# Attention block on one core: softmax sums by 32x32 block transposes, 1/l broadcast through memory, first loads in another order

## The chip, the cores and the metric

One core of a Trainium2 chip runs the whole kernel. The metric is the device time of one execution in microseconds (us), the median of several. Engines are named as in the profile: PE (TensorE matmul), PEld (its weight loads), DVE (VectorE), ACT (ScalarE), POOL (GpSimd), SP (SyncE, here the queue that issues most DMAs).

## The reference

The input x is 16 images of 512 channels by 32x32 = 1024 positions, float32 throughout. For each image:

```
xn   = groupnorm(x; 8 groups) * gamma + beta
q,k,v = qkv_w @ xn + qkv_b            (4 heads of 128 channels)
attn = softmax_m(q^T k / sqrt(128))   (1024 x 1024 per head)
o    = attn @ v
out  = x + proj_w @ o + proj_b
```

## The kernel before, in words

Channels lie on the 128 partitions, positions along the free axis, so an image is four tiles x_b_0..3 of 128x1024. Every product is float32 with 512 moving columns; one such call appears in the trace as two MATMUL records.

The program is unrolled over `steps` = 16 images x 4 heads x 8 blocks of 128 keys. Step s computes in `scores` (L243) a score block of 128 keys x 1024 queries (two calls, L247), its exponential p on ACT (L252), and adds p to a running sum `tot` on DVE (L255, L257). In the same step `weighted_sum` (L274) adds the block before, s-1, into `po` in PSUM (L280). The softmax maximum is not subtracted; a flag computed at the end says whether the sums stayed in a safe range, and a slower general path runs only if they did not.

At the first step of the next head, `denominators` (L259) takes `tot` (128 keys-within-block x 1024 queries) and sums it over the partitions. It does so with a product against a 128x128 tile of ones (L264), two halves, so that the sum l of every query stands on all 128 partitions. DVE then computes 1/l on 128x512 twice (L266) and a check value `worst` twice (L269). When the last key block has been added, DVE multiplies `po` by 1/l into `o` (L288), which frees `po`.

`plan_head` (L309) spreads other work over a head's steps: the q and k products of the next head (`qk_unit`, L204), in head 0 the output projection of the image before (`proj_unit`, L226, from step 2) and the loads of the next image, in head 2 the group statistics of the next image (L38 to L64), in head 3 its normalisation (L69 on DVE, then the beta addition L72 on POOL, on DVE for the first image), its q, k of head 0 and its v (L216).

The Tile framework does not keep this order on each engine: it puts every engine's instructions in order when the kernel is built, from priorities that follow the order of the code and from its own estimate of when each is ready. An engine then runs its list strictly in that order. Tiles come from pools; PSUM has two score tiles of two banks (`ps_s`), one `po` of two banks (`ps_o`) and two one-bank accumulators (`ps_a`, tag acc) that q/k, v, projection and l all share.

At the start the four x tiles of image 0 are issued on SP's queue, gamma, beta and all weights (four tiles of 768 KB for q, k and v, then the projection) on ACT's queue. At the end come the flag and the eight projection units of the last image.

Of the kernel before, what the change touches and what calls it, by code (L numbers as in the profile page):

```python
# [26 lines left out]
class Norm:  # L27
# [36 lines left out]
        nc.vector.tensor_mul(sc, rstd, self.gamma)  # L64
        return mu, sc

    def apply(self, xn, x, mu, sc, c, eng):

        self.nc.vector.tensor_scalar(  # L69
            xn, x, mu[:, c : c + 1], sc[:, c : c + 1], ALU.subtract, ALU.mult  # L70
        )
        eng.tensor_scalar(xn, xn, self.beta[:, c : c + 1], None, ALU.add)  # L72


@with_exitstack
def attention_block(
    ctx: ExitStack,
    tc: tile.TileContext,
    x: bass.AP,
    gamma: bass.AP,  # L80
    beta: bass.AP,
    qkv_wT: bass.AP,
    qk_b: bass.AP,
    v_b: bass.AP,
    proj_wT: bass.AP,
    proj_b: bass.AP,
    out: bass.AP,
):
# [12 lines left out]
    avg = const.tile([P, P], F32, name="avg")  # L101
    neghalf = const.tile([P, NCC], F32, name="neghalf")
    ones = const.tile([P, P], F32, name="ones")
# [5 lines left out]
    wqkv = [const.tile([P, 3 * C], F32, name=f"wqkv_{c}") for c in range(NCC)]  # L109
    wproj = [const.tile([P, C], F32, name=f"wproj_{c}") for c in range(NCC)]  # L110

    spans = const.tile([P, B * HEADS * NH2], F32, name="spans")
    flag = const.tile([P, 1], I32, name="flag")

    with ExitStack() as fast:
        fast_path(
            fast, tc, x, (gamma, beta, qkv_wT, qk_b, v_b, proj_wT, proj_b), out,
            avg, neghalf, ones, gamma_sb, beta_sb, qkb_sb, vb_sb, projb_sb, wqkv, wproj,
            spans, flag, (B, C, N, NCC, NH2, NB, GC, SCALE),
        )  # L120
# [11 lines left out]
def fast_path(  # L132
    ctx, tc, x, sources, out, avg, neghalf, ones, gamma_sb, beta_sb, qkb_sb, vb_sb, projb_sb,
    wqkv, wproj, spans, flag, dims,
):

# [37 lines left out]
    nc.scalar.dma_start(vb_sb, v_b.to_broadcast((P, C)))  # L174
# [13 lines left out]

    def normalise(b, c):
        xns[b, c] = xnpool.tile([P, N], F32, tag="xn", name=f"xn_{b}_{c}")  # L190
        norm.apply(xns[b, c], xs[b, c], *scaled[b], c, nc.vector if b == 0 else nc.gpsimd)


    def qk_unit(b, h, which, half):

        store = (qs, ks)[which]
        if half == 0:
            store[b, h] = qkpool.tile(
                [P, N], F32, tag=f"qk{which}", name=f"qk{which}_{b}_{h}"
            )  # L200
        o = which * HEADS + h
        acc = ps_a.tile([P, HALF], F32, tag="acc", name=f"pqk_{b}_{h}_{which}_{half}")
        for c in range(NCC):
            nc.tensor.matmul(  # L204
                acc, wqkv[c][:, ts(o, P)], xns[b, c][:, ts(half, HALF)],
                start=(c == 0), stop=(c == NCC - 1),
            )
        nc.scalar.activation(  # L208
            store[b, h][:, ts(half, HALF)], acc, AF.Identity, bias=qkb_sb[:, o : o + 1]
        )  # L210

    def v_unit(b, j):

        acc = ps_a.tile([P, HALF], F32, tag="acc", name=f"pv_{b}_{j}")
        for c in range(NCC):
            nc.tensor.matmul(  # L216
                acc[:, :C], xns[b, c][:, ts(j, P)], wqkv[c][:, 2 * C : 3 * C],
                start=(c == 0), stop=(c == NCC - 1),
            )
# [3 lines left out]
    def proj_unit(b, o, half):  # L223
        acc = ps_a.tile([P, HALF], F32, tag="acc", name=f"pp_{b}_{o}_{half}")
        for c in range(NCC):
            nc.tensor.matmul(  # L226
                acc, wproj[c][:, ts(o, P)], os_[b, c][:, ts(half, HALF)],
                start=(c == 0), stop=(c == NCC - 1),
            )
        y = ypool.tile([P, HALF], F32, tag="y", name=f"y_{b}_{o}_{half}")  # L230
# [12 lines left out]
    def scores(s):  # L243
# [8 lines left out]
        nc.scalar.activation(ps[s], sc, AF.Exp, scale=SCALE)  # L252
# [6 lines left out]
    def denominators(b, h):  # L259

        t = tot.pop((b, h))
        for half in range(NH2):
            l = ps_a.tile([P, HALF], F32, tag="acc", name=f"l_{b}_{h}_{half}")
            nc.tensor.matmul(l, ones, t[:, ts(half, HALF)], start=True, stop=True)  # L264
            r = lpool.tile([P, HALF], F32, tag=f"rinv{half}", name=f"rinv_{b}_{h}_{half}")
            nc.vector.reciprocal(r, l)  # L266
            worst = lpool.tile([P, HALF], F32, tag="worst", name=f"worst_{b}_{h}_{half}")
            i = (b * HEADS + h) * NH2 + half
            nc.vector.scalar_tensor_tensor(  # L269
                worst, l, 1.0, r, ALU.mult, ALU.max, accum_out=spans[:, i : i + 1]  # L270
            )
            rinv[b, h, half] = r

    def weighted_sum(s):  # L274
        b, h, j = where(s)
# [68 lines left out]
    for s in range(steps + 1):  # L344
        if s < steps:
# [11 lines left out]
    total = gn.tile([P, 1], F32, tag="total", name="total")  # L357
    nc.vector.tensor_reduce(total, spans, AX.X, ALU.add)
    fine = gn.tile([P, 1], F32, tag="fine", name="fine")
    nc.vector.tensor_scalar(fine, total, LIMIT, None, ALU.is_le)  # L360
    nc.vector.tensor_scalar(flag, fine, -1.0, 1.0, ALU.mult, ALU.add)
    for u in proj_units(B - 1):
        u()


def general_path(
# [21 lines left out]
    with tc.For_i(0, B, 1) as b:  # L388
# [8 lines left out]
            norm.chunk(mv, xs[c], c)  # L397
        mu, sc = norm.group(mv)
        for c in range(NCC):
            norm.apply(xn[c], xs[c], mu, sc, c, nc.vector)  # L400
        for j in range(NB):
            acc = product(lambda c: xn[c][:, ts(j, P)], lambda c: wqkv[c][:, 2 * C : 3 * C])
            nc.vector.tensor_add(vs[j], acc, vb_sb)
        for h in range(HEADS):
            for w in range(2):
                i = w * HEADS + h
                for half in range(NH2):
                    acc = product(
                        lambda c: wqkv[c][:, ts(i, P)], lambda c: xn[c][:, ts(half, HALF)]
                    )  # L410
                    nc.scalar.activation(
                        q[w][:, ts(half, HALF)], acc, AF.Identity, bias=qkb_sb[:, i : i + 1]
# [76 lines left out]
```

## Time and profile before

| | us |
|---|---|
| median of 3 runs | 3697.14 (3696.3 to 3697.45) |
| the profiled execution's own time | 3696.41 |
| its span in the trace | 3694.5 |

| engine | busy us | share of the span |
|---|---|---|
| PE | 3654.3 | 99% |
| PEld | 1608.1 | 44% |
| DVE | 1470.9 | 40% |
| ACT | 701.1 | 19% |
| POOL | 200.2 | 5% |

The span begins with the first instruction of any engine and ends with the last. A PE record's time is modelled to its pipelined end, so records of a stream overlap: the time between starts tells what one costs.

### The profile page before, as it was taken

What the parts mean: (1) busy time and instruction counts of PE and PEld (TensorE: products, weight loads), DVE (VectorE), ACT (ScalarE), POOL (GpSimd) and SP (SyncE); (2) the same over time, 40 slices, a digit from 0 to 9 for tenths busy, and PEclk for the clock granted to TensorE, in tenths of its full rate; (3) what the DMA queues carried; (4) which work ended last, traced back from release to release, by engine and by line L of the source; (5) the groups of instructions that cost most, each with busy time, mean ns of one, the idle gap of its engine ahead of it and who ended that gap; (6) DMA issues with size and microseconds to landing.
All of it is one profiled execution on the core that took longest, in us unless ns stands there. A gap on an engine that the chain in (4) does not pass through costs nothing.

```text
span 3694.5 us, 20904 instructions
## 1 busy us (share of the span) xinstructions
PE 3654.3 (99%) x8512; PEld 1608.1 (44%) x8512; DVE 1470.9 (40%) x1596; ACT 701.1 (19%) x769; POOL 200.2 (5%) x80
## 2 busy tenths in 40 slices
PE   7999999999999999999999999999999999999998
PEld 3444444444444444444444444444444444444443
DVE  3334434434344343433434334353434434344334
ACT  1211212112121121211212112121211212112121
POOL 0010100101001010000101001010010100101000
PEclk9999999999999999999999999999999999999999
DMA  2001010010100101001010010100001000010000
GB/s 94 0 0 46 0 37 9 0 46 0 41 5 3 43 0 46 0 10 36 0 46 0 12 35 0 46 0 15 31 0 46 0 23 23 0 46 0 14 9 24
DMA packets 29621, 72.97 MB, mean 20 GB/s; under 512 B 3792, under 2 KB 3792, under 8 KB 29520
## 3 DMA queue, kind: packets, MB, share of 16 engines
q1 hardware_dynamic: 27648, 67.12, 5.3%
q10 hardware_dynamic: 1872, 4.47, 0.3%
q8 instruction: 68, 1.11, 0.1%
q14 instruction: 33, 0.27, 0.0%
HBM read 38.02 MB, written 33.55 MB: 19 GB/s over the span
## 4 chain that ended last, share of the span: by engine, by line
PE 92%; DVE 2%; POOL 0%; issue 0%; POOLq 0%
PE pqk L204 22%; PE po L280 22%; PE s L247 21%; PE pp L226 12%; PE pv L216 11%; PE l L264 3%; DVE xn L69 2%; DVE tot L257 0%; POOL rstd L62 0%; DVE rinv L266 0%; PE pv L58 0%; DVE sc L64 0%; DVE ve L60 0%; PE pm L47 0%; DVE y L231 0%
## 5 line engine op out<-in xcount | busy, mean ns | idle before, releaser
L280 PE MATMUL po<-p,v 128*128 128x512 f32 x2048 | 961.6, 593 | 0.0
L257 DVE TENSOR_TENSOR tot<-tot,p 128x1024 f32<-128x1024 f32 x384 | 470.2, 1225 | 1233.0 <-ACT p L252 1219.1
L247 PE MATMUL s<-qk,qk 128*128 128x512 f32 x2048 | 941.6, 592 | 0.0
L204 PE MATMUL pqk<-xn,wqkv 128*128 128x512 f32 x2048 | 925.4, 593 | 4.3 <-DVE xn L72 4.3
L252 ACT ACTIVATE p<-s 128x1024 f32<-128x1024 f32 x512 | 523.9, 1023 | 1949.5 <-PE s L247 1947.1
L204 PEld LDWEIGHTS pqk<-xn,wqkv 128*128 128x128 f32 x2048 | 389.9, 190 | 495.2 <-issue 474.9
L247 PEld LDWEIGHTS s<-qk,qk 128*128 128x128 f32 x2048 | 389.1, 190 | 489.8 <-issue 474.5
L280 PEld LDWEIGHTS po<-p,v 128*128 128x128 f32 x2048 | 386.8, 190 | 475.5 <-issue 456.1
L266 DVE RECIPROCAL rinv<-l 128x512 f32<-128x512 f32 x128 | 420.4, 3326 | 301.3 <-PE l L264 301.3
L226 PE MATMUL pp<-o,wproj 128*128 128x512 f32 x1024 | 457.3, 595 | 5.5 <-DVE worst L269 5.5
L216 PE MATMUL pv<-wqkv,xn 128*128 128x512 f32 x1024 | 449.4, 592 | 0.0
L208 ACT ACTIVATE qk<-pqk,qkb_sb 128x512 f32<-128x512 f32 x256 | 175.9, 687 | 978.6 <-PE pqk L204 978.6
L226 PEld LDWEIGHTS pp<-o,wproj 128*128 128x128 f32 x1024 | 195.6, 191 | 252.5 <-issue 241.7
L216 PEld LDWEIGHTS pv<-wqkv,xn 128*128 128x128 f32 x1024 | 194.6, 190 | 244.9 <-issue 244.9
L221 DVE TENSOR_TENSOR v<-pv,vb_sb 128x512 f32<-128x512 f32 x128 | 88.5, 691 | 266.7 <-PE pv L216 266.7
L62 POOL TENSOR_TENSOR rstd<-ve,neghalf 128x4 f32<-128x4 f32 x16 | 16.6, 1035 | 3183.6 <-DVE ve L60 3183.6
L72 POOL TENSOR_SCALAR xn<-xn,beta_sb 128x1024 f32<-128x1024 f32 x60 | 183.5, 3072 | 19.0 <-DVE xn L69 16.1
L231 DVE SCALAR_TENSOR_TENSOR y<-pp,projb_sb,x 128x512 f32<-128x512 f32 x128 | 95.4, 745 | 218.1 <-PE pp L226 218.1
L38 DVE BATCH_NORM_STATS2 st<-x 128x6 f32<-128x512 f32 x128 | 82.3, 683 | 143.4 <-DMA x<-in_x 143.4
L264 PE MATMUL l<-tot,ones 128*128 128x512 f32 x256 | 130.7, 618 | 6.1 <-DVE tot L257 6.1
L288 DVE TENSOR_TENSOR o<-po,rinv 128x512 f32<-128x512 f32 x128 | 82.1, 683 | 0.0
L255 DVE TENSOR_TENSOR tot<-p,p 128x1024 f32<-128x1024 f32 x64 | 77.8, 1216 | 7.2 <-ACT p L252 7.2
(29 smaller groups left out, 252.5 us busy)
## 6 DMA issues: line engine op xcount, KB each, us to landing
x<-in_x SPq DMA_DIRECT2D x64, 512.0 KB, 3.8
out_y<-y SPq DMA_DIRECT2D x128, 256.0 KB, 2.0
wqkv<-in_qkv_wT ACTq DMA_DIRECT2D x4, 768.0 KB, 9.8
wproj<-in_proj_wT ACTq DMA_DIRECT2D x4, 256.0 KB, 6.5
vb_sb<-in_v_b ACTq DMA_DIRECT2D x1, 256.0 KB, 11.4
gamma_sb<-in_gamma ACTq DMA_DIRECT2D x1, 2.0 KB, 4.3
beta_sb<-in_beta ACTq DMA_DIRECT2D x1, 2.0 KB, 5.2
qkb_sb<-in_qk_b ACTq DMA_DIRECT2D x1, 4.0 KB, 6.0
```

The source lines that it names most:

```text
L72: eng.tensor_scalar(xn, xn, self.beta[:, c : c + 1], None, ALU.add)
L204: nc.tensor.matmul(acc, wqkv[c][:, ts(o, P)], xns[b, c][:, ts(half, HALF)], start=(c == 0), stop=(c == NCC - 1),)
L208: nc.scalar.activation(store[b, h][:, ts(half, HALF)], acc, AF.Identity, bias=qkb_sb[:, o : o + 1])
L216: nc.tensor.matmul(acc[:, :C], xns[b, c][:, ts(j, P)], wqkv[c][:, 2 * C : 3 * C], start=(c == 0), stop=(c == NCC - 1),)
L226: nc.tensor.matmul(acc, wproj[c][:, ts(o, P)], os_[b, c][:, ts(half, HALF)], start=(c == 0), stop=(c == NCC - 1),)
L231: nc.vector.scalar_tensor_tensor(y, acc, projb_sb[:, o : o + 1], xs[b, o][:, ts(half, HALF)], ALU.add, ALU.add)
L247: nc.tensor.matmul(sc[:, ts(half, HALF)], ks[b, h][:, ts(j, P)], qs[b, h][:, ts(half, HALF)], start=True, stop=True,)
L252: nc.scalar.activation(ps[s], sc, AF.Exp, scale=SCALE)
L257: nc.vector.tensor_add(tot[b, h], tot[b, h], ps[s])
L264: nc.tensor.matmul(l, ones, t[:, ts(half, HALF)], start=True, stop=True)
L266: nc.vector.reciprocal(r, l)
L280: nc.tensor.matmul(po[b, h][:, ts(half, HALF)], vs[b, j][:, ts(h, P)], p[:, ts(half, HALF)], start=(j == 0), stop=(j == NB - 1),)
```

## The change

Four things are edited.

1. **Sums.** `denominators` no longer multiplies by ones. DVE transposes `tot` in 32x32 blocks (one instruction on 128x1024), sums each block's rows (one reduction, 128x32x32 to 128x32), and PE adds the four partition groups with a product of 32x32 outputs. 1/l and the check run on 32x32. The 1024 values are written to a row in memory by SP's queue and read back, broadcast to 128 partitions (512 KB), by the same queue.
2. **Division.** ACT copies `po` to `o` as soon as the last block is in; DVE divides `o` in place (`divide`, one 128x1024 product) at step 1 of the next head. The projection of the image before starts at step 3 of head 0. At the end, three of the four terms of six projection units are computed ahead of the last division.
3. **Beta.** For images after the first the beta addition moves from POOL to ACT.
4. **Loads.** x of image 0 goes over SP's and ACT's queues in turn; the q, k, v weights become separate 128x512 tiles, q and v on SP's queue, k on ACT's. The loads of the next image wait for an exponential of step 7 of head 0.

```
-        for half in range(NH2):
-            l = ps_a.tile([P, HALF], F32, tag="acc", name=f"l_{b}_{h}_{half}")
-            nc.tensor.matmul(l, ones, t[:, ts(half, HALF)], start=True, stop=True)
-            r = lpool.tile([P, HALF], F32, tag=f"rinv{half}", name=f"rinv_{b}_{h}_{half}")
-            nc.vector.reciprocal(r, l)
...
+        tt = lpool.tile([P, N // BLK, BLK], F32, tag="tt", name=f"tt_{b}_{h}")
+        nc.vector.transpose(tt.rearrange("p c m -> p (c m)"), t)
+        part = lpool.tile([P, N // BLK], F32, tag="part", name=f"part_{b}_{h}")
+        nc.vector.tensor_reduce(part, tt, AX.X, ALU.add)
+        l = ps_a.tile([P, HALF], F32, tag="acc", name=f"l_{b}_{h}")
+        nc.tensor.matmul(l[:BLK, :BLK], part, fold, start=True, stop=True)
+        r = lpool.tile([BLK, BLK], F32, tag="r", name=f"r_{b}_{h}")
+        nc.vector.reciprocal(r, l[:BLK, :BLK])
...
+        row = dpool.tile([1, N], F32, tag="row", name=f"row_{b}_{h}")
+        nc.sync.dma_start(row.rearrange("o (c i) -> (o c) i", i=BLK), r)
+        rinv[b, h] = lpool.tile([P, N], F32, tag="rinv", name=f"rinv_{b}_{h}")
+        nc.sync.dma_start(rinv[b, h], row.to_broadcast((P, N)))
...
         if j == NB - 1:
-            o = po.pop((b, h))
             os_[b, h] = opool.tile([P, N], F32, tag="o", name=f"o_{b}_{h}")
-            for half in range(NH2):
-                nc.vector.tensor_mul(
-                    os_[b, h][:, ts(half, HALF)], o[:, ts(half, HALF)], rinv.pop((b, h, half))
-                )
+            nc.scalar.copy(os_[b, h], po.pop((b, h)))
+
+    def divide(b, h):
+        nc.vector.tensor_mul(os_[b, h], os_[b, h], rinv.pop((b, h)))
...
-                spread(plan, proj_units(b - 1), 2, 7)
+                spread(plan, proj_units(b - 1), 3, 7)
...
+            if j == 1 and s > NB:
+                divide(*where(s - NB)[:2])
...
-        eng.tensor_scalar(xn, xn, self.beta[:, c : c + 1], None, ALU.add)
+        if on_scalar:
+            nc.scalar.activation(xn, xn, AF.Identity, bias=beta)
...
-            nc.sync.dma_start(xs[b, c], x[b, ts(c, P), :])
+            eng = (nc.sync, nc.scalar)[c % 2] if b == 0 else nc.sync
+            dma = eng.dma_start(xs[b, c], x[b, ts(c, P), :])
+            if last_exp:
+                tc.add_manual_dep(
...
-    nc.vector.memset(ones, 1.0)
+    make_identity(nc, fold[0:BLK, :])
+    for a in range(1, P // BLK):
+        nc.vector.tensor_copy(fold[ts(a, BLK), :], fold[0:BLK, :])
...
-    for c in range(NCC):
-        nc.scalar.dma_start(wqkv[c], qkv_wT[ts(c, P), :])
+    for n in range(3):
+        for c in range(NCC):
+            eng = (nc.sync, nc.scalar)[n % 2]
+            eng.dma_start(wqkv[n][c], qkv_wT[ts(c, P), ts(n, C)])
...
+    early = [(o, half) for o in range(3) for half in range(NH2)]
...
+    for acc, (o, half) in zip(accs, early):
+        proj_products(acc, B - 1, o, half, range(NCC - 1))
+    divide(B - 1, HEADS - 1)
+    for acc, (o, half) in zip(accs, early):
+        proj_products(acc, B - 1, o, half, [NCC - 1])
+        proj_store(acc, B - 1, o, half)
```

The flag's last steps change with it: the check values are summed over 32 partitions by one more tiny product, ahead of the last two projection units.

## Rows read from the trace of the kernel before

**Rows 1.** The page: busy us of each engine, share of the span, instructions.

```profile
PE 3654.3 (99%) x8512; PEld 1608.1 (44%) x8512; DVE 1470.9 (40%) x1596; ACT 701.1 (19%) x769; POOL 200.2 (5%) x80
```

**Rows 2.** One image's period by windows: length, busy us of each engine, granted clock.

```profile
437.36:665.79 228.43, 228.02 (x534) 100.35 (x533) 91.80 (x100) 43.73 (x48) 13.29 (x5) 1.00 0.06 19
```

**Rows 3.** Groups by line: shapes and count, busy us, mean ns, idle before and its releaser.

```profile
L264 PE MATMUL l<-tot,ones 128*128 128x512 f32 x256 | 130.7, 618 | 6.1 <-DVE tot L257 6.1
...
L257 DVE TENSOR_TENSOR tot<-tot,p 128x1024 f32<-128x1024 f32 x384 | 470.2, 1225 | 1233.0 <-ACT p L252 1219.1 <-DVE tot L255 0.5 <-DVE tot L257 0.5
...
L266 DVE RECIPROCAL rinv<-l 128x512 f32<-128x512 f32 x128 | 420.4, 3326 | 301.3 <-PE l L264 301.3
...
L252 ACT ACTIVATE p<-s 128x1024 f32<-128x1024 f32 x512 | 523.9, 1023 | 1949.5 <-PE s L247 1947.1 <-PE po L280 2.4
```

**Rows 4.** The chain of waits through one image: start us, us, work, records.

```profile
417.21 0.12 PE pm L47 x2
...
418.29 0.28 PE pv L58 x2
...
499.23 1.90 PE l L264 x4
...
612.90 1.90 PE l L264 x4
```

**Rows 5.** Timeline where head 3 begins: start us, us, engine, line, [idle before].

```profile
417.96 0.16 DVE L56 TENSOR_TENSOR vv<-d,mv 128x4 f32<-128x4 f32 x1
...
420.18 3.78 DVE L69 TENSOR_SCALAR xn<-x,mu,sc 128x1024 f32<-128x1024 f32 x4
...
422.79 1.88 PE L247 MATMUL s<-qk,qk 128*128 128x512 f32 x4
423.88 1.21 DVE L257 TENSOR_TENSOR tot<-tot,p 128x1024 f32<-128x1024 f32 x1
...
425.14 1.98 PE L264 MATMUL l<-tot,ones 128*128 128x512 f32 x4 [0.47 <-DVE tot L257]
...
426.96 1.88 PE L280 MATMUL po<-p,v 128*128 128x512 f32 x4
428.68 5.31 PE L247 MATMUL s<-qk,qk 128*128 128x512 f32 x12
```

**Rows 6.** Timeline where head 2 begins.

```profile
378.63 1.22 DVE L257 TENSOR_TENSOR tot<-tot,p 128x1024 f32<-128x1024 f32 x1 [5.64 <-ACT p L252]
...
384.25 2.07 PE L264 MATMUL l<-tot,ones 128*128 128x512 f32 x4
...
385.31 6.57 DVE L266 RECIPROCAL rinv<-l 128x512 f32<-128x512 f32 x2 [5.45 <-PE l L264]
```

**Rows 7.** Timeline of the start.

```profile
12.95 1.29 DVE L38 BATCH_NORM_STATS2 st<-x 128x6 f32<-128x512 f32 x2 [3.78 <-DMA x<-in_x]
...
18.81 0.69 DVE L38 BATCH_NORM_STATS2 st<-x 128x6 f32<-128x512 f32 x1 [1.08 <-DMA x<-in_x]
19.42 0.14 DVE L56 TENSOR_TENSOR vv<-d,mv 128x4 f32<-128x4 f32 x1
...
24.48 16.33 PE L204 MATMUL pqk<-xn,wqkv 128*128 128x512 f32 x32 [4.27 <-DVE xn L72]
```

**Rows 8.** Timeline of the end, PE.

```profile
3652.08 1.02 PE L280 MATMUL po<-p,v 128*128 128x512 f32 x2
...
3658.60 30.60 PE L226 MATMUL pp<-o,wproj 128*128 128x512 f32 x64 [5.50 <-DVE worst L269]
```

**Rows 9.** The end by windows: columns as in rows 2.

```profile
3650.30:3694.50 44.20, 33.40 (x71) 14.19 (x70) 15.44 (x19) 0.00 (x0) 0.00 (x0) 0.89 0.13 49
```

**Rows 10.** DMA issues by line, count, KB each, median us to landing; then x's extremes.

```profile
x<-in_x SPq DMA_DIRECT2D x64, 512.0 KB, 3.8
out_y<-y SPq DMA_DIRECT2D x128, 256.0 KB, 2.0
...
DMA to landing us min/median/max: 3.5/3.8/12.8
```

More of the change, by code (lines that the diff above doesn't have):

```diff
@@ L20 @@
 EPS = 1e-5
+BLK = 32
 HALF = 512
@@ L65, in group, with apply @@
         return mu, sc
-    def apply(self, xn, x, mu, sc, c, eng):
-        self.nc.vector.tensor_scalar(
+    def apply(self, xn, x, mu, sc, c, on_scalar):
+        nc, beta = self.nc, self.beta[:, c : c + 1]
+        nc.vector.tensor_scalar(
             xn, x, mu[:, c : c + 1], sc[:, c : c + 1], ALU.subtract, ALU.mult
         )
-        eng.tensor_scalar(xn, xn, self.beta[:, c : c + 1], None, ALU.add)
+        if on_scalar:
+            nc.scalar.activation(xn, xn, AF.Identity, bias=beta)
+        else:
+            nc.vector.tensor_scalar(xn, xn, beta, None, ALU.add)
 @with_exitstack
@@ L102, in attention_block @@
     neghalf = const.tile([P, NCC], F32, name="neghalf")
-    ones = const.tile([P, P], F32, name="ones")
+    fold = const.tile([P, BLK], F32, name="fold")
     gamma_sb = const.tile([P, NCC], F32, name="gamma_sb")
@@ L108, in attention_block @@
     projb_sb = const.tile([P, NCC], F32, name="projb_sb")
-    wqkv = [const.tile([P, 3 * C], F32, name=f"wqkv_{c}") for c in range(NCC)]
+    wqkv = [
+        [const.tile([P, C], F32, name=f"w{n}_{c}") for c in range(NCC)] for n in "qkv"
+    ]
     wproj = [const.tile([P, C], F32, name=f"wproj_{c}") for c in range(NCC)]
-    spans = const.tile([P, B * HEADS * NH2], F32, name="spans")
-    flag = const.tile([P, 1], I32, name="flag")
+    spans = const.tile([BLK, B * HEADS], F32, name="spans")
+    flag = const.tile([1, 1], I32, name="flag")
     with ExitStack() as fast:
@@ L117, in attention_block @@
             fast, tc, x, (gamma, beta, qkv_wT, qk_b, v_b, proj_wT, proj_b), out,
-            avg, neghalf, ones, gamma_sb, beta_sb, qkb_sb, vb_sb, projb_sb, wqkv, wproj,
+            avg, neghalf, fold, gamma_sb, beta_sb, qkb_sb, vb_sb, projb_sb, wqkv, wproj,
             spans, flag, (B, C, N, NCC, NH2, NB, GC, SCALE),
@@ L132, in fast_path @@
 def fast_path(
-    ctx, tc, x, sources, out, avg, neghalf, ones, gamma_sb, beta_sb, qkb_sb, vb_sb, projb_sb,
+    ctx, tc, x, sources, out, avg, neghalf, fold, gamma_sb, beta_sb, qkb_sb, vb_sb, projb_sb,
     wqkv, wproj, spans, flag, dims,
@@ L148, in fast_path @@
     lpool = ctx.enter_context(tc.tile_pool(name="l", bufs=2))
+    dpool = ctx.enter_context(tc.tile_pool(name="rows", bufs=4, space=bass.MemoryType.DRAM))
     ypool = ctx.enter_context(tc.tile_pool(name="y", bufs=3))
@@ L156, in fast_path @@
     mvs, scaled = {}, {}
+    last_exp = []
     def load_x(b):
@@ L160, in load_x @@
             xs[b, c] = xpool.tile([P, N], F32, tag="x", name=f"x_{b}_{c}")
-            nc.sync.dma_start(xs[b, c], x[b, ts(c, P), :])
+            eng = (nc.sync, nc.scalar)[c % 2] if b == 0 else nc.sync
+            dma = eng.dma_start(xs[b, c], x[b, ts(c, P), :])
+            if last_exp:
+                tc.add_manual_dep(
+                    dma.ins, last_exp[0].name,
+                    mybir.DependencyInfo(
+                        mybir.DependencyClass.Sync, mybir.DependencyReason.DATA
+                    ),
+                    reason="not before the image in work needs no more of the start",
+                )
     load_x(0)
@@ L167, in fast_path @@
     nc.vector.memset(neghalf, -0.5)
-    nc.vector.memset(ones, 1.0)
+    make_identity(nc, fold[0:BLK, :])
+    for a in range(1, P // BLK):
+        nc.vector.tensor_copy(fold[ts(a, BLK), :], fold[0:BLK, :])
+    fold_ones = gn.tile([BLK, 1], F32, tag="fold_ones", name="fold_ones")
+    nc.vector.memset(fold_ones, 1.0)
     nc.scalar.dma_start(gamma_sb, gamma)
@@ L190, in normalise @@
         xns[b, c] = xnpool.tile([P, N], F32, tag="xn", name=f"xn_{b}_{c}")
-        norm.apply(xns[b, c], xs[b, c], *scaled[b], c, nc.vector if b == 0 else nc.gpsimd)
+        norm.apply(xns[b, c], xs[b, c], *scaled[b], c, b > 0)
     def qk_unit(b, h, which, half):
@@ L204, in qk_unit @@
             nc.tensor.matmul(
-                acc, wqkv[c][:, ts(o, P)], xns[b, c][:, ts(half, HALF)],
+                acc, wqkv[which][c][:, ts(h, P)], xns[b, c][:, ts(half, HALF)],
                 start=(c == 0), stop=(c == NCC - 1),
@@ L216, in v_unit @@
             nc.tensor.matmul(
-                acc[:, :C], xns[b, c][:, ts(j, P)], wqkv[c][:, 2 * C : 3 * C],
+                acc[:, :C], xns[b, c][:, ts(j, P)], wqkv[2][c],
                 start=(c == 0), stop=(c == NCC - 1),
@@ L221, in v_unit, with proj_products @@
         nc.vector.tensor_add(vs[b, j], acc[:, :C], vb_sb)
-    def proj_unit(b, o, half):
-        acc = ps_a.tile([P, HALF], F32, tag="acc", name=f"pp_{b}_{o}_{half}")
-        for c in range(NCC):
+    def proj_products(acc, b, o, half, chunks):
+        for c in chunks:
             nc.tensor.matmul(
@@ L229, in proj_unit, with proj_store @@
             )
+    def proj_store(acc, b, o, half):
         y = ypool.tile([P, HALF], F32, tag="y", name=f"y_{b}_{o}_{half}")
@@ L234, in proj_unit @@
         nc.sync.dma_start(out[b, ts(o, P), ts(half, HALF)], y)
+    def proj_unit(b, o, half):
+        acc = ps_a.tile([P, HALF], F32, tag="acc", name=f"pp_{b}_{o}_{half}")
+        proj_products(acc, b, o, half, range(NCC))
+        proj_store(acc, b, o, half)
     ps, tot, po, rinv = {}, {}, {}, {}
@@ L251, in scores @@
         ps[s] = ppool.tile([P, N], F32, tag="p", name=f"p_{s}")
-        nc.scalar.activation(ps[s], sc, AF.Exp, scale=SCALE)
+        e = nc.scalar.activation(ps[s], sc, AF.Exp, scale=SCALE)
+        last_exp[:] = [e.ins]
         if j == 1:
@@ L261, in denominators @@
         t = tot.pop((b, h))
-        for half in range(NH2):
-            l = ps_a.tile([P, HALF], F32, tag="acc", name=f"l_{b}_{h}_{half}")
-            nc.tensor.matmul(l, ones, t[:, ts(half, HALF)], start=True, stop=True)
-            r = lpool.tile([P, HALF], F32, tag=f"rinv{half}", name=f"rinv_{b}_{h}_{half}")
-            nc.vector.reciprocal(r, l)
[L267 to L270, printed above, removed]
-            )
-            rinv[b, h, half] = r
+        tt = lpool.tile([P, N // BLK, BLK], F32, tag="tt", name=f"tt_{b}_{h}")
[6 more added lines that the diff above has]
+        nc.vector.reciprocal(r, l[:BLK, :BLK])
+        worst = lpool.tile([BLK, BLK], F32, tag="worst", name=f"worst_{b}_{h}")
+        i = b * HEADS + h
+        nc.vector.scalar_tensor_tensor(
+            worst, l[:BLK, :BLK], 1.0, r, ALU.mult, ALU.max, accum_out=spans[:, i : i + 1]
+        )
+        row = dpool.tile([1, N], F32, tag="row", name=f"row_{b}_{h}")
+        nc.sync.dma_start(row.rearrange("o (c i) -> (o c) i", i=BLK), r)
+        rinv[b, h] = lpool.tile([P, N], F32, tag="rinv", name=f"rinv_{b}_{h}")
+        nc.sync.dma_start(rinv[b, h], row.to_broadcast((P, N)))
     def weighted_sum(s):
@@ L355, in fast_path @@
             weighted_sum(s - 1)
-    total = gn.tile([P, 1], F32, tag="total", name="total")
+    early = [(o, half) for o in range(3) for half in range(NH2)]
+    wide = [ps_s.tile([P, N], F32, tag="s", name=f"pp_last_{i}") for i in range(2)]
+    accs = [wide[i // NH2][:, ts(i % NH2, HALF)] for i in range(2 * NH2)]
+    accs += [
+        ps_a.tile([P, HALF], F32, tag="acc", name=f"pp_last_{i}")
+        for i in range(len(accs), len(early))
+    ]
+    for acc, (o, half) in zip(accs, early):
[4 more added lines that the diff above has]
+        proj_store(acc, B - 1, o, half)
+    total = gn.tile([BLK, 1], F32, tag="total", name="total")
     nc.vector.tensor_reduce(total, spans, AX.X, ALU.add)
-    fine = gn.tile([P, 1], F32, tag="fine", name="fine")
-    nc.vector.tensor_scalar(fine, total, LIMIT, None, ALU.is_le)
+    most = ps_o.tile([P, N], F32, tag="o", name="most")
+    nc.tensor.matmul(most[:1, :1], total, fold_ones, start=True, stop=True)
+    fine = gn.tile([1, 1], F32, tag="fine", name="fine")
+    nc.vector.tensor_scalar(fine, most[:1, :1], LIMIT, None, ALU.is_le)
     nc.vector.tensor_scalar(flag, fine, -1.0, 1.0, ALU.mult, ALU.add)
-    for u in proj_units(B - 1):
-        u()
+    for half in range(NH2):
+        proj_unit(B - 1, NCC - 1, half)
 def general_path(
@@ L399, in general_path @@
         for c in range(NCC):
-            norm.apply(xn[c], xs[c], mu, sc, c, nc.vector)
+            norm.apply(xn[c], xs[c], mu, sc, c, False)
         for j in range(NB):
-            acc = product(lambda c: xn[c][:, ts(j, P)], lambda c: wqkv[c][:, 2 * C : 3 * C])
+            acc = product(lambda c: xn[c][:, ts(j, P)], lambda c: wqkv[2][c])
             nc.vector.tensor_add(vs[j], acc, vb_sb)
@@ L408, in general_path @@
                     acc = product(
-                        lambda c: wqkv[c][:, ts(i, P)], lambda c: xn[c][:, ts(half, HALF)]
+                        lambda c: wqkv[w][c][:, ts(h, P)], lambda c: xn[c][:, ts(half, HALF)]
                     )
```

3 lines of the change are left out of this document (1 added, 2 removed).

## The prediction

> **What bounds the kernel now.** I read the page's busy shares first: PE is busy for 99% of the span and no other engine for half of it [rows 1]. [...] The spacing of starts gives the price of a record: four records of `po` at 426.96 are followed by scores at 428.68, 1.72 us later [rows 5], so 0.429 us a record. PE is the bound from about 25 us to the end, and time falls only by PE work removed, by PE waits removed, or at the two ends, where PE stands still. The groups then give the product against ones: 256 records, 130.7 us busy, only 6.1 us of idle time before them [rows 3]. The chain says what that product costs a head: 1.90 us in three heads of an image (first and last of the three shown) [rows 4], and in the fourth from the end of the scores at 422.79 + 1.72 = 424.51 to the next `po` at 426.96, which is 2.45 us, a wait for `tot` included [rows 5].
>
> **The change part by part, against the profiled execution's 3696.4 us (span 3694.5); the median of the runs is 0.7 us above it.**
>
> *The product against ones goes.* 3 x 1.90 + 2.45 = 8.15 us an image, x 16 = 130.4 us, which agrees with the group's 130.7 [rows 3 to 5]. All of it is on the path, since PE has nothing to wait for around it.
>
> *A tiny product comes* (weights 128x32, 32 columns), 64 of them. The trace has two tiny products, `pm` and `pv`, 128 weight columns and 4 moving columns, each between large ones: 0.12 and 0.28 us in the chain [rows 4]. I take 0.25 us, near the dearer, since it has 32 columns: 64 x 0.25 = 16 us. Bounds: 64 x 0.12 = 8 us, and the 0.63 us that PE stood before the `l` at 425.14 (424.51 to 425.14) as a price for each, 40 us [rows 5].
>
> [...] No row has a 32-column load, and I stay with `pv`.
>
> *The chain to that product becomes longer.* Where `l` waited for `tot`, it now waits for `tot`, a transpose and a reduction. Neither is in the trace. The nearest row in shape is the DVE addition on 128x1024, 1.22 us; the slowest DVE kind is the reciprocal, 3.33 us for 512 columns, so 6.65 for 1024 [rows 3]. I take 1.22 each, 2.5 us together. Behind the waiting product on PE stand `po` of the last block and all that follows. In three heads the cover is there: at head 2 the last addition ends at 379.85 and `l` starts at 384.25, 4.4 us of PE work in between, and DVE idles 5.45 us before its reciprocal [rows 6]. At head 3 there is none: `tot` ends at 425.09 and `l` starts at once [rows 5]. But `po` (1.72) and the next scores (1.72) do not depend on `l`, and the framework moves ready work ahead: the four normalisations that the code has in steps 0 and 1 of head 3 run at 420.18, before the `tot` of the last step of head 2, and three steps of scores run in one piece at 428.68 [rows 5]. So I expect those 3.4 us to be put in front and cost this wait at nothing. Without it the wait is 0.6 + 2.5 us once an image: 50 us.
>
> *1/l, check, copy, division.* DVE loses 2 x 3.33 us of reciprocals a head and more, and gains about 2.5 + 1.2 us [rows 3]; it was not the bound. The gain for PE is small and is in the 8.15 already. ACT gains a 128x1024 copy a head and four beta additions an image, about 1.02 us each as the exponential [rows 3]: 8.2 us on top of 43.73 busy out of 228 [rows 2]. It costs nothing as long as exponentials stay ahead of `po`; where head 3 begins, five exponentials and five of these passes are 10 us against some 17 us of PE work.
>
> *Through memory.* A row write and a 512 KB broadcast, one behind the other on SP's queue. Nearest rows: a store lands in 2.0 us, a 512 KB load in 3.8 [rows 10]: 5.8 us, some 7 with issue, after `l`. `divide` stands after step 1, at the least 1.72 + 1.72 us of PE work plus an exponential and an addition (1.02 + 1.22), 5.7 us after `l`. So DVE may stand for 1 to 2 us at `divide`; behind it are the additions to `tot` and evictions of v, which start only at step 3, and PE waits for neither that soon. Price nothing; the projection's shift from step 2 to 3 gives head 0 the same cover. SP's queue also holds the four loads of the next image, now in one bunch at step 7 of head 0, and a row write behind them. That head's broadcast may be late by the largest landing, 12.8 us [rows 10], once an image, still ahead of head 2.
>
> *Start.* PE's stream begins at 24.48. The fourth x tile's statistics begin at 12.95 after a wait for its load, and are done about 1.5 us later; then `vv`, which in a quiet image follows `pm` by 0.75 us [rows 4, 5], comes at 19.42, because statistics of image 1 stand in between and wait for their loads (18.81) [rows 7]. With loads of image 1 held back, 14.5 to 19.4 shrinks to about 1.5 us: 3.4 us. x in front of the weights on two queues may bring the fourth tile earlier, at most 3.8 us, DVE's wait before it [rows 7]. I take 6 us together. Bounds: 7.2 us, and below nothing, a loss of 3 us, if DVE's copies of `fold`, queued before the statistics, wait for POOL to build it.
>
> *End.* PE stands from 3652.08 + 2 x 0.429 = 3652.94 to 3658.60, 5.66 us, and then its 64 records take 30.60 instead of 27.5 us, at a mean granted clock of 0.89 in the stretch [rows 8, 9]. After the change 18 products of early terms (36 x 0.429 = 15.4 us) cover transpose, reduction, both transfers and the division (about 11 us). 5.7 + 3.1 - 0.3 for the flag's tiny product = 8.5 us; at worst nothing.
>
> Sum: 3696.4 - 130.4 + 16 - 6 - 8.5 = 3567.5, and 0.7 for the median: **3568 us**.
>
> **Rivals.**
>
> *A: `l` stands where it stood at head 3.* The framework's estimate makes it ready too early, and PE waits 3.1 us an image: 3568 + 50 = 3618 us. For it: that `l` already waits for `tot` [rows 5]; against it: the moved work in the same rows.
>
> *B, the other side: the transpose is slow.* At the reciprocal's pace, 6.65 us, the chain is 7.9 us. In three heads it passes the cover of 4.4 by 3.5, at head 3 the 3.4 us of `po` and scores by 4.5: 15 us an image, 240 us, so 3808 us. It decides against the change from 129 / 64 = 2.0 us of standing PE a head, a transpose of about 5 us. [...]
>
> *C: the broadcast comes late every head.* If it takes the 12.8 us of the slowest x load [rows 10], `divide` holds DVE for some 9 us a head. PE runs on for as long as p has buffers (four, some 3 steps of 3.4 us), so perhaps 1 us a head is left: 3568 + 64 = 3632 us.
>
> *D: PE's removed time is only passed on to another engine.* Then nothing changes, 3697. Against it: no other engine is above 44% [rows 1].
>
> **How the numbers follow.** The forecast 0.81, A 0.09, C 0.04, B 0.05, D 0.01. About 0.2% is what a measurement of this kernel can tell from no change. The forecast, A and C are faster: 0.94; D same, 0.01; B slower, 0.05. The range: down to 3552 (tiny product at 8 us, the start's 7.2 and a few us of less friction at `po`), up to 3620 (A, or the tiny product at 40 us with no gain at the start).
>
> **What would show it.** The image period falls from 228.43 to about 221.3 at a granted clock of 1.00. L264's 512-column records are gone, and the tiny product costs PE 0.1 to 0.3 us. Transpose and reduction show 1.2 us each; 5 us means B. At head 3 `po` and scores stand ahead of `l`; idle PE before `l` of over 1 us means A. PE's stream begins near 18 us and runs without a gap through the last projection. I am wrong if PE's idle time within a period grows above its 0.4 us by more than 1 us, or if DVE's wait at `divide` reaches PE through v's or the projection's evictions.

## The result, and the profile after

The changed kernel takes 3592.27 us (median of four runs, 3590.52 to 3592.37), the kernel before 3696.72 in the same comparison: a ratio of 0.9717, 95% interval 0.970 to 0.9733. Forecast were 3568 us within 3552 to 3620. The sign, the place and the range held; of 128.9 us forecast, 104.3 came (span 3694.5 to 3590.2).

The page of the changed kernel, busy us by engine, beside [rows 1]:

```profile
PE 3555.8 (99%) x8386; PEld 1567.8 (44%) x8386; DVE 1150.2 (32%) x1471; ACT 824.6 (23%) x893; POOL 16.6 (0%) x22
```

PE is as full as before, with less to do. One image's period and the stretch of PE's last 16 records, by windows (columns as in [rows 2]):

```profile
412.75:635.34 222.59, 221.90 (x525) 97.86 (x525) 71.57 (x91) 51.71 (x57) 1.01 (x1) 1.00 0.08 29
3576.33:3585.14 8.81, 8.77 (x16) 3.60 (x16) 1.35 (x3) 0.00 (x0) 0.00 (x0) 0.81 0.34 123
```

A period is 228.43 - 222.59 = 5.84 us shorter, where 7.15 were forecast; 16 of them make 93.4 us. The new operations and their waits, by groups (L298 transpose, L300 reduction, L302 the tiny product, L330 the division):

```profile
L298 DVE STREAM_TRANSPOSE tt<-tot 128x1024 f32<-128x1024 f32 x64 | 79.7, 1245 | 2.2
...
L300 DVE TENSOR_REDUCE part<-tt 128x32 f32<-128x1024 f32 x64 | 78.1, 1220 | 2.2
...
L330 DVE TENSOR_TENSOR o<-o,rinv 128x1024 f32<-128x1024 f32 x64 | 78.1, 1220 | 9.9 <-DMA rinv<-row 9.8
L75 ACT ACTIVATE xn<-xn,beta_sb 128x1024 f32<-128x1024 f32 x60 | 65.5, 1139 | 45.8 <-DVE xn L71 45.8
...
L302 PE MATMUL l<-fold,part 128*32 128x32 f32 x128 | 15.9, 206 | 10.2 <-DVE part L300 10.2
...
rinv<-row SPq DMA_DIRECT2D x64, 512.0 KB, 3.5
```

Transpose (1.245 us) and reduction (1.220) take what the addition takes (1.225 [rows 3]), as forecast. The broadcast (last row, a DMA issue: KB each, median us to landing) keeps DVE waiting 9.8 us in all, and no wait of PE comes from it: the way through memory costs nothing. What one tiny product costs PE in heads 0 to 2, the spacing of starts shows:

```profile
548.17 3.60 PE L231 MATMUL pqk<-xn,wq 128*128 128x512 f32 x8
551.69 0.25 PE L302 MATMUL l<-fold,part 128*32 128x32 f32 x2
551.87 1.98 PE L321 MATMUL po<-p,v 128*128 128x512 f32 x4
553.69 1.88 PE L280 MATMUL s<-qk,qk 128*128 128x512 f32 x4
```

The eight records before it end at 548.17 + 8 x 0.429 = 551.60, so the product begins 0.09 us late, takes 0.18 to the next start, and the four records behind it take 1.82 instead of 1.72: 0.38 us together (0.376 before rounding).

Besides, PE idles 10.2 us before the tiny product. Where, the timeline at the start of head 3 shows, beside [rows 5] and a row of the kernel before, the first score record of step 7 there:

```profile
419.36 1.88 PE L247 MATMUL s<-qk,qk 128*128 128x512 f32 x4
```

The changed kernel:

```profile
626.76 1.88 PE L280 MATMUL s<-qk,qk 128*128 128x512 f32 x4
...
627.54 2.98 DVE L71 TENSOR_SCALAR xn<-x,mu,sc 128x1024 f32<-128x1024 f32 x4
628.39 2.19 ACT L75 ACTIVATE xn<-xn,beta_sb 128x1024 f32<-128x1024 f32 x2 [3.05 <-DVE xn L71]
...
630.49 1.00 ACT L285 ACTIVATE p<-s 128x1024 f32<-128x1024 f32 x1
...
631.52 1.23 DVE L291 TENSOR_TENSOR tot<-tot,p 128x1024 f32<-128x1024 f32 x1 [1.00 <-ACT p L285]
...
633.63 1.02 PE L280 MATMUL s<-qk,qk 128*128 128x512 f32 x2
634.06 1.22 DVE L300 TENSOR_REDUCE part<-tt 128x32 f32<-128x1024 f32 x1
...
635.34 0.25 PE L302 MATMUL l<-fold,part 128*32 128x32 f32 x2 [0.69 <-DVE part L300]
```

Compared with the order before, the framework put `po` and half of the next scores ahead of the product, 6 records or 2.58 us. Still PE stands from 633.63 + 0.86 to 635.34, 0.85 us, and it does so in 15 of the 16 images; the last image has no next one to normalise. Two beta passes on ACT stand before the exponential of step 7, and four normalisations on DVE before the addition. The exponential is the later of the two: the normalisations end at 630.52, and DVE then idles 1.00 us for it.

The start, PE's stream at 18.19 instead of 24.48 [rows 7]:

```profile
11.25 0.64 DVE L39 BATCH_NORM_STATS2 st<-x 128x6 f32<-128x512 f32 x1
...
13.61 0.16 DVE L57 TENSOR_TENSOR vv<-d,mv 128x4 f32<-128x4 f32 x1
...
18.19 9.49 PE L231 MATMUL pqk<-xn,wq 128*128 128x512 f32 x16 [3.78 <-DMA wproj<-in_proj_wT]
```

(The product does not read `wproj`, which its row names; the weight load beside it waits 3.87 us for the beta addition on DVE.)

The end, PE and the two lines of DVE that matter, beside [rows 8]; an eviction is DVE's pass (L259) that takes a finished unit out of PSUM:

```profile
3554.76 18.29 PE L252 MATMUL pp_last<-o,wproj 128*128 128x512 f32 x42
...
3573.70 1.12 PE L252 MATMUL pp_last<-o,wproj 128*128 128x512 f32 x2 [0.53 <-DVE fine L419]
...
3574.86 2.07 DVE L259 SCALAR_TENSOR_TENSOR y<-pp_last,projb_sb,x 128x512 f32<-128x512 f32 x3 [0.99 <-PE pp_last L252]
...
3576.33 8.77 PE L252 MATMUL pp<-o,wproj 128*128 128x512 f32 x16 [1.50 <-DVE y L259]
...
3585.14 0.75 DVE L259 SCALAR_TENSOR_TENSOR y<-pp,projb_sb,x 128x512 f32<-128x512 f32 x1 [2.68 <-PE pp L252]
```

The stand of 5.5 us before the projection is gone, but a new one of 1.50 us precedes the last two units, and their 16 records take 8.77 us, at a mean granted clock of 0.81; behind the same stand they take 7.13 in another run of this series (e6). From the end of the last `po` to the start of the last eviction it was 36.30 us before (3652.94 to 3689.24) and is 32.37 now (3552.77 to 3585.14): 3.9 us, not 8.5.

### The profile page after: what moved, and what is told of

Read it like the earlier page. It is cut to its first block, busy times and chain, and to the rows that moved or that the text cites. A ratio compares the mean times of both kernels' runs of the same rounds, so it can differ in the third digit from the quotient of the medians.

```text
span 3590.2 us, 20812 instructions
## 1 busy us (share of the span) xinstructions
PE 3555.8 (99%) x8386; PEld 1567.8 (44%) x8386; DVE 1150.2 (32%) x1471; ACT 824.6 (23%) x893; POOL 16.6 (0%) x22
## 4 chain that ended last, share of the span: by engine, by line
PE 95%; DVE 2%; ACT 1%; DMA 0%; POOL 0%; issue 0%; SPq 0%; POOLq 0%
PE pqk L231 25%; PE po L321 23%; PE s L280 23%; PE pv L243 12%; PE pp L252 12%; ACT xn L75 1%; PE pp_last L252 1%; DVE tt L298 1%; DVE tot L291 1%; DVE part L300 1%; POOL rstd L63 0%; ACT p L285 0%; PE l L302 0%; DVE xn L71 0%; DMA wq<-in_qkv_wT 0%
## 5 line engine op out<-in xcount | busy, mean ns | idle before, releaser
L231 PE MATMUL pqk<-xn,wq 128*128 128x512 f32 x1024 | 460.2, 595 | 3.8 <-DMA wproj<-in_proj_wT 3.8
L231 PE MATMUL pqk<-xn,wk 128*128 128x512 f32 x1024 | 457.7, 592 | 0.0
L243 PE MATMUL pv<-wv,xn 128*128 128x512 f32 x1024 | 449.4, 592 | 0.0
L252 PE MATMUL pp<-o,wproj 128*128 128x512 f32 x976 | 430.6, 594 | 1.5 <-DVE y L259 1.5
L231 PEld LDWEIGHTS pqk<-xn,wq 128*128 128x128 f32 x1024 | 195.4, 191 | 249.7 <-issue 245.3
L231 PEld LDWEIGHTS pqk<-xn,wk 128*128 128x128 f32 x1024 | 194.6, 190 | 244.9 <-issue 244.9
L243 PEld LDWEIGHTS pv<-wv,xn 128*128 128x128 f32 x1024 | 194.6, 190 | 244.9 <-issue 244.9
L259 DVE SCALAR_TENSOR_TENSOR y<-pp,projb_sb,x 128x512 f32<-128x512 f32 x122 | 91.6, 751 | 236.7 <-PE pp L252 236.7
L330 DVE TENSOR_TENSOR o<-o,rinv 128x1024 f32<-128x1024 f32 x64 | 78.1, 1220 | 9.9 <-DMA rinv<-row 9.8
L327 ACT COPY o<-po 128x1024 f32<-128x1024 f32 x64 | 64.6, 1009 | 69.1 <-PE po L321 69.1
L298 DVE STREAM_TRANSPOSE tt<-tot 128x1024 f32<-128x1024 f32 x64 | 79.7, 1245 | 2.2
```

What stands on the lines that cost most here:

```text
L231: nc.tensor.matmul(acc, wqkv[which][c][:, ts(h, P)], xns[b, c][:, ts(half, HALF)], start=(c == 0), stop=(c == NCC - 1),)
L243: nc.tensor.matmul(acc[:, :C], xns[b, c][:, ts(j, P)], wqkv[2][c], start=(c == 0), stop=(c == NCC - 1),)
L252: nc.tensor.matmul(acc, wproj[c][:, ts(o, P)], os_[b, c][:, ts(half, HALF)], start=(c == 0), stop=(c == NCC - 1),)
L259: nc.vector.scalar_tensor_tensor(y, acc, projb_sb[:, o : o + 1], xs[b, o][:, ts(half, HALF)], ALU.add, ALU.add)
L298: nc.vector.transpose(tt.rearrange("p c m -> p (c m)"), t)
```

## The experiments

Differences between kernels are taken from medians of four runs each (3592.3 us for the changed kernel), places from the traces. The kernel before, measured again beside the experiments, came to 3696.1 us instead of 3696.7, so a difference of 0.6 us says nothing.

**Beta back on POOL (e1).**

```
-            nc.scalar.activation(xn, xn, AF.Identity, bias=beta)
+            nc.gpsimd.tensor_scalar(xn, xn, beta, None, ALU.add)
```

> The beta addition of later images goes back from ACT to POOL; all else as in the changed kernel, where at the start of head 3 the tiny product begins 8.58 us after the first score record of step 7 and PE stands 0.85 us before it. Theory A (ACT's beta passes hold up the exponential of step 7, and with it the last addition, transpose and reduction): the product's operand comes about 1.8 us earlier, so the product begins under 7.3 us after that record, no wait is left, and the time falls by 13 us to about 3579. Rival (DVE's four normalisations stand ahead of the addition anyway): the addition still begins when they end, and they run at 0.99 instead of 0.75 to 0.81 us beside POOL, so the product begins 8.2 to 8.6 us after the record; the framework has put it one pair of score products earlier, so PE stands 0.8 to 1.7 us and the time stays or rises by up to 14 us, 3590 to 3606.

3599.24 us, ratio to before 0.9736 (0.972 to 0.9753). The rival holds:

```profile
628.67 1.88 PE L280 MATMUL s<-qk,qk 128*128 128x512 f32 x4
...
629.42 3.78 DVE L71 TENSOR_SCALAR xn<-x,mu,sc 128x1024 f32<-128x1024 f32 x4
...
630.59 1.02 ACT L285 ACTIVATE p<-s 128x1024 f32<-128x1024 f32 x1 [3.34 <-PE s L280]
...
633.13 1.21 DVE L291 TENSOR_TENSOR tot<-tot,p 128x1024 f32<-128x1024 f32 x1
...
633.82 1.88 PE L321 MATMUL po<-p,v 128*128 128x512 f32 x4
...
636.93 0.25 PE L302 MATMUL l<-fold,part 128*32 128x32 f32 x2 [1.23 <-DVE part L300]
```

The exponential now runs at once and ends at 631.61, yet the addition waits 1.5 us more, until the fourth normalisation has ended. The product begins 636.93 - 628.67 = 8.26 us after the first score record, 8.58 in the changed kernel. So ACT's passes are not the cause alone: here the normalisations, which are longer beside POOL's passes (0.995 us on the mean, 0.809 in the changed kernel), are what the addition waits for, while in the changed kernel it is the exponential behind ACT's passes. The move to ACT gains 6.9 us, but not through an earlier operand, which comes 0.32 us later with it. It gains by the place of the product: in the changed kernel two more score records (0.86 us) stand in front, so that PE stands 0.85 us an image, where it stands 636.93 - (633.82 + 1.72) = 1.39 here. Why the framework chose the other place was not looked into.

**Normalisations behind the sums (e2).** The four DVE passes get an ordering edge to the reduction of head 2 (an order on DVE, no wait), and are planned in step 1.

```
-                spread(plan, [lambda c=c: normalise(b + 1, c) for c in range(NCC)], 0, 2)
+                spread(plan, [lambda c=c: normalise(b + 1, c) for c in range(NCC)], 1, 2)
...
+        if after is not None:
+            self.hold(t.ins, after)
```

> The normalisations of the next image are ordered behind the reduction of head 2's sums on DVE, so neither DVE's passes nor ACT's beta passes stand ahead of exponential, addition, transpose and reduction at the start of head 3. Both theories of what stands in front (ACT's beta passes or DVE's normalisations) expect the operand to be ready about 6.7 us after the first score record of step 7, the wait of 0.85 us an image to go, and 13 us less: 3579. Rival (the chain of exponential, addition, transpose and reduction is too long by itself): the wait stays, 3592. A third outcome: normalisation now comes late for the q products two steps later, PE waits there, and the time rises by up to 16 times the delay.

3579.94 us, ratio to before 0.9685 (0.9669 to 0.9701): 12.3 us less, 13 were expected.

```profile
624.42 1.88 PE L294 MATMUL s<-qk,qk 128*128 128x512 f32 x4
...
627.39 1.22 DVE L305 TENSOR_TENSOR tot<-tot,p 128x1024 f32<-128x1024 f32 x1 [2.23 <-ACT p L299]
...
631.07 0.80 DVE L71 TENSOR_SCALAR xn<-x,mu,sc 128x1024 f32<-128x1024 f32 x1
631.38 0.25 PE L317 MATMUL l<-fold,part 128*32 128x32 f32 x2
...
636.81 7.03 PE L245 MATMUL pqk<-xn,wq 128*128 128x512 f32 x16
```

The addition begins 2.97 us after the first score record (4.76 in the changed kernel), the product 6.96 us after it with no wait, and the q product that needs all four normalised tiles does not wait either. The edit moves DVE's passes and, with them, ACT's beta passes, which need their results; it does not tell the two apart.

**Two tiny products (e4).** The second copy is not used.

```
+        nc.tensor.matmul(l[:BLK, BLK : 2 * BLK], part, fold, start=True, stop=True)
         nc.tensor.matmul(l[:BLK, :BLK], part, fold, start=True, stop=True)
```

> The tiny product is issued twice, side by side in the same bank; the second copy is not used. In the changed kernel one costs PE 0.38 us in heads 0 to 2: 0.18 itself and 0.10 on either side of it. If the two 0.10 belong to going from a large product to a tiny one and back, the second copy costs 0.18 us: 64 x 0.18 = 11.5 us, 3604. If each tiny product costs 0.38 us, 24 us: 3616. [...]

3595.99 us, ratio to before 0.9727 (0.9711 to 0.9744): 3.7 us more, 0.06 us a copy, below both prices expected (0.18 and 0.38).

```profile
552.75 0.25 PE L302 MATMUL l<-fold,part 128*32 128x32 f32 x2
552.83 0.23 PE L303 MATMUL l<-fold,part 128*32 128x32 f32 x2
552.99 1.98 PE L322 MATMUL po<-p,v 128*128 128x512 f32 x4
```

From start to start the two take 0.08 and 0.16 us; in the changed kernel one takes 0.18. So of the 0.38 us that one costs PE, about 0.06 is its own and 0.32 the passage from large products to a tiny one and back.

**No tiny product (e9, on e2 and e3 together).** Four small DMAs bring the partition groups side by side, DVE adds them.

```
+        four = lpool.tile([BLK, P // BLK, N // BLK], F32, tag="four", name=f"four_{b}_{h}")
+        for a in range(P // BLK):
+            nc.sync.dma_start(four[:, a, :], part[ts(a, BLK), :])
...
-        nc.tensor.matmul(l[:BLK, :BLK], part, fold, start=True, stop=True)
+        nc.vector.tensor_reduce(l, four.rearrange("i a c -> i c a"), AX.X, ALU.add)
...
+        nc.vector.transpose(r, ri)
```

> The kernel with both gains, but PE makes no tiny product: the four 32-partition groups of the row sums are brought side by side by four small DMAs on SP's queue, DVE adds them, and a 32x32 transpose puts the reciprocals in the order of the row in memory. Theory: the tiny product costs PE 0.38 us a head, 0.06 itself and 0.32 for standing between large ones, and taking it away gives 64 x 0.38 = 24 us: 3551. The chain to 1/l grows by a DMA of about 2 us and two small DVE passes; the division then waits on DVE, but PE needs it only from step 3 of head 0. Rival: DVE, standing at the division for 2 to 4 us a head, holds up additions, so that exponential buffers or accumulators come free late and PE stands 0.4 us or more a head: 3575 or slower.

3553.16 us, ratio to before 0.9614 (0.9598 to 0.963), the fastest of all: 23.6 us less than the same kernel with the tiny product, 0.37 us a head. Its waits (us in total, times, the longest):

```profile
DVE o L350 <- ACT o L347: 101.0, 15, 6.9
DVE l L320 <- DMA four<-part: 85.4, 35, 3.8
DVE o L350 <- DMA rinv<-row: 72.0, 33, 5.1
```

DVE stands longer (85.4 us for the small DMAs; at the division 72.0 for the broadcast and 101.0 for ACT's copy, in total), and PE does not notice: its period is 220.33 us (from `pm` at 398.35 to `pm` at 618.68), 512 records at 0.429 us and 0.66 us for the two tiny products of the group statistics, `pm` and `pv`.

**Order of the last accumulators (e3).**

```
-    accs = [wide[i // NH2][:, ts(i % NH2, HALF)] for i in range(2 * NH2)]
-    accs += [
+    accs = [
         ps_a.tile([P, HALF], F32, tag="acc", name=f"pp_last_{i}")
-        for i in range(len(accs), len(early))
+        for i in range(2 * NH2, len(early))
     ]
+    accs += [wide[i // NH2][:, ts(i % NH2, HALF)] for i in range(2 * NH2)]
```

> Of the six early projection units at the end, the first two get the one-bank accumulators that the last two units need, and the other four the score tiles; before, it was the last two. Theory: PE's stand of 1.5 us before the last two units, and their 16 records at 8.77 instead of 6.87 us after it, come from the accumulators being freed last in DVE's order. Expect both to go: the last eviction starts 3 to 3.5 us earlier, 3589 in all. Rival (the stand comes from the division or from the flag's product): the stand stays, 3592.

3587.82 us, ratio to before 0.9707 (0.9691 to 0.9724): 4.4 us less. The stand and the slow records are gone, and from the end of the last `po` (3552.27) to the last eviction it is 28.41 us, 7.9 less than before the change:

```profile
3573.55 1.88 PE L252 MATMUL pp<-o,wproj 128*128 128x512 f32 x4
...
3576.18 4.46 PE L252 MATMUL pp<-o,wproj 128*128 128x512 f32 x10
...
3580.68 0.75 DVE L259 SCALAR_TENSOR_TENSOR y<-pp,projb_sb,x 128x512 f32<-128x512 f32 x1 [2.68 <-PE pp L252]
```

Of the 4.4 us some 1.6 are the slow records, and these do not always come with the stand (e6 below); the stands of 0.53 and 1.50 us are most of the rest.

**Both (e5).** Only the edits of e2 and e3.

> Normalisations behind head 2's sums and the new order of the last accumulators together. If the two gains are in different places, as both traces show, they add: 12.3 and 4.4 us off 3592.3, so 3575.5, between 3574 and 3577. If the earlier end of an image moves work that the tail's order relied on, only part of the 4.4 is left: 3577 to 3580.

3576.74 us (3576.17 to 3577.61), ratio to before 0.9678 (0.9661 to 0.9694): 15.5 of the 16.7 us. The 1.2 us that are missing are less than the 1.9 us by which the four runs of the changed kernel lie apart, so this does not tell whether all of the sum came.

**Image 1 not held back (e6).**

```
-        last_exp[:] = [e.ins]
+        last_exp[:] = [e.ins] if b > 0 else []
```

> Only the wait is taken out that holds image 1's loads until an exponential of image 0; x and weights keep their new order. In the changed kernel PE's stream begins at 18.2 us, before the change at 24.5. If holding image 1 back is what counts, the stream begins about 3.4 us later, at 21 to 22; if it is x ahead of the weights on two queues, it stays within 1 us of 18.2.

One run, 3590.61 us. The stream begins at 18.38, with the wait at 18.19; SP issues image 1's loads at 15.73, behind the weights.

```profile
15.73 3.04 SPq L174 DMA_DIRECT2D x<-in_x  x4
...
18.38 9.11 PE L231 MATMUL pqk<-xn,wq 128*128 128x512 f32 x16 [3.78 <-DMA wproj<-in_proj_wT]
...
3576.17 7.13 PE L252 MATMUL pp<-o,wproj 128*128 128x512 f32 x16 [1.50 <-DVE y L259]
```

So the wait does nothing at the start: image 1's loads, behind the weights on the same queue, are late enough without it. What x on two queues adds by itself was not tried.

The last row is the end of this run: PE stands 1.50 us as in the changed kernel, and the 16 records behind it take 7.13 us, not 8.77.

**Four transposes (e7).**

```
-        nc.vector.transpose(tt.rearrange("p c m -> p (c m)"), t)
+        for _ in range(4):
+            nc.vector.transpose(tt.rearrange("p c m -> p (c m)"), t)
```

> The transpose is done four times over (the same result), so the chain from the last addition to the tiny product is 6.2 instead of 2.5 us, as if one transpose took 5 us; this is the changed kernel of the prediction otherwise. Theory of the prediction's rival B: PE stands 1.8 us in three heads and 2.8 us in head 3, where it stood 0.85; the time rises by some 16 x (3 x 1.8 + 2.0) = 118 us, to 3710, and the change is lost. Rival: the framework, which knows of the four, moves the tiny product behind other ready products in every head, PE stands no longer than it did, and the time stays within 15 us of 3592.

3604.39 us, ratio to before 0.9753 (0.9737 to 0.977): 12.1 us more, not 118.

```profile
597.50 0.25 PE L303 MATMUL l<-fold,part 128*32 128x32 f32 x2 [0.17 <-DVE part L301]
...
642.67 0.25 PE L303 MATMUL l<-fold,part 128*32 128x32 f32 x2 [1.03 <-DVE part L301]
```

The framework moves the product behind more ready work: between the first transpose and the product PE starts 18, 14, 13 and 26 records in the four heads of an image, where it started 10, 10, 3 and 26. PE stands 1.19 us at head 3 and 0.32 at head 2, counted by starts as the 0.85 above (1.03 and 0.17 in the rows, which count from the modelled end of the record before).

## Why the prediction was right, and where its sizes were off

*The product against ones: right.* It was worth 8.15 us an image. The tiny product in its place costs 3 x 0.38 in heads 0 to 2, and at head 3 the wait of 0.85 and 0.28 of its own: 2.27 us. The difference, 5.88, is the 5.84 us by which the period fell.

*The tiny product: under-sized.* "I take 0.25 us, near the dearer": measured 0.38 in 49 heads and 0.28, beside the wait, in 15; both lie inside the bounds of 0.12 and 0.63. That is 22.8 us instead of 16, 6.8 lost. `pv`, the row that I took, was read from the chain, where it shows 0.28; the spacing of starts adds what the large products on either side lose (0.66 us for `pm` and `pv` together in e9's period, where the chain has 0.40). By itself the product costs less than I took, 0.06 for the second copy of e4; for a lone one among large ones the trace has 0.38, and for the sum that decides.

*The cover at head 3: wrong by 0.85 us in 15 images, 12.8 in all.* This is the step that failed. "So I expect those 3.4 us to be put in front and cost this wait at nothing": 2.58 us were put in front, `po` and half of the next scores. And 3.43 us were to be covered, not 3.1: the product begins 8.58 us after the first score record of step 7, and before the change PE was free for `l` 424.51 - 419.36 = 5.15 us after it. Of the 0.33 us more, 0.24 is a later start of the last addition, 4.76 us after that record instead of 423.88 - 419.36 = 4.52.

The four normalisations that I cited as a sign of moved work [rows 5] stand ahead of that addition themselves, before the change and after it; with the beta passes on ACT, which hold the exponential, they cost it 4.76 - 2.97 = 1.8 us, as e2 shows, where all of them are behind and the wait is gone. How the 1.8 us divide is not shown by a run: e1 takes ACT's passes away but makes the normalisations longer, and ACT's passes alone were not moved. By the rows of the changed kernel the exponential behind ACT's passes is the later by 1.00 us, more than the wait of 0.85. Rival A came true on a small scale: the product was put where its operand was not ready, 0.85 us too early and not 3.1.

*Beta on ACT: priced at nothing.* It delays the exponential of step 7 by 1.8 us (3.73 us after the first score record, 1.92 in e1). Still it is worth 6.9 us against POOL by e1, through the place that the framework gave the product, which I had not considered.

*Through memory: right.* The broadcast lands in 3.5 us, and DVE waits 9.8 us over 64 heads. Rival C did not occur.

*The start: 6.3 us against 6.* The 3.4 us came: from the end of image 0's last statistics to `vv` it was 19.42 - 14.24 = 5.18 us [rows 7] and is 13.61 - 11.89 = 1.72, since image 1's statistics no longer stand in between; these statistics also end 2.4 us earlier. But I gave this to the wait that holds image 1 back, and e6 shows the order of the queue enough.

*The end: 3.9 us against 8.5.* The early products cover the division as worked out. What I left out was who frees the accumulators: the last two units need those of units 4 and 5, whose evictions stand last in DVE's list, behind the flag; each score tile is one tile for two units, so its second unit's last term waits for the first unit's eviction. PE stood 0.53 and 1.50 us, and in the profiled execution its last 16 records then took 1.6 us more than in e6. e3 gives back 4.4 us.

*The sum.* 6.8 for the own cost of the tiny products, 12.8 for the wait, 4.6 at the end and -0.3 at the start make 23.9 of the 24.6 us that were missing; the other 0.7 I have not followed. That 3592 us lies inside the range is owed to its upper end, which was set for rival A in full or a tiny product of 0.63 us, and not to a reckoning of these terms together.

*Rival B* did not occur: the transpose takes 1.245 us, near the addition's 1.225, and not the 6.65 of the reciprocal's pace. And e7 shows its price wrong tenfold for a slowness that the framework knows when it orders the work. What a slowness unknown to it costs was not tried, nor were stands of B's size, 3.5 to 4.5 us a head, and what clock would follow them. D was excluded by the profile.

## What to carry to other kernels

PE was 99% busy here, and 5.88 us an image of work and waits less took 5.84 us off the period. The tiny product put in is priced by what it takes from the spacing of the starts around it, 0.38 us, and not by its own duration, 0.25 for its two records. When a chain that PE waits for grows longer, look at what stands ahead of its first link on every engine of the chain (1.8 us here), do not count moved work as cover before asking what it was moved ahead of, and count the cover in records of the new order once there is one (2.58 us here, for 3.43). At the end of a kernel, follow each buffer to the instruction that frees it (PE stood 0.53 and 1.50 us here).

## What the runs showed of the hardware that was not expected

- One product of 32 columns among products of 512 costs PE 0.38 us, a second beside it 0.06 (e4). Four small DMAs and two DVE passes in its place cost PE nothing that shows: taking 64 products away gave 23.6 us, 0.37 each (e9).
- A normalisation pass on DVE (128x1024) takes 0.995 us on the mean with POOL's beta passes beside it (e1) and 0.809 with ACT's. It is the third of an image's four passes that takes longer, 1.61 us; the others take some 0.81, as with ACT. The kernel before, with its beta passes on POOL too, shows the same pass by pass: of the four at 420.18 [rows 5] the third begins at 421.63 and takes 1.60 us, the fourth at 423.15 and takes 0.80, and both lie within POOL's first pass (421.19, 3.66 us). So a pass beside POOL's took twice its time or no longer than without; what decides is not shown. The groups with POOL's passes (e1) and with ACT's (the changed kernel), the last bar being idle time before them, and e1's passes as ns at least, median, at most:

```profile
L71 DVE TENSOR_SCALAR xn<-x,mu,sc 128x1024 f32<-128x1024 f32 x64 | 59.8, 995 | 0.6
...
L71 DVE TENSOR_SCALAR xn<-x,mu,sc 128x1024 f32<-128x1024 f32 x64 | 47.8, 809 | 0.6
...
L71 DVE TENSOR_SCALAR xn<-x,mu,sc x64: 801/811/1615, 16.1 to 3309.9; 128x1024 f32<-128x1024 f32 x64
```

- Near the end, behind the same stand of PE of 1.50 us, the last 16 records took 8.77 us in the profiled execution of the changed kernel, with a mean granted clock of 0.81 over 8.81 us (0.55 up to 3580.00, 1.00 from there). In e6's they took 7.13. In the groups, where the idle time before them is 1.5 us each time, the projection's `pp` records (976, these 16 among them) are busy 430.6 us in all in the changed kernel's execution, 430.6 in e2's and 430.4 in e4's, but 428.9 in e1's. So these records may or may not be slower behind such a stand, by some 1.6 us here; the lower clock was read in the changed kernel alone, and what decides is not shown.
